# Moving the first image's VectorE work in a fused convolution and attention block

## The chip, the cores and the metric

The kernel runs on one core of one Trainium2 chip. The metric is the device time of one execution in microseconds (us). TensorE (PE in the profile) does the matmuls, VectorE (DVE) the additions, ScalarE (ACT) the activations and copies out of PSUM, GpSimd (POOL) and SyncE (SP) mostly issue transfers.

## The reference, cut to what matters

Eight images of 512 channels by 32x32 pixels, all in f32. Each is group-normalised, goes through one block and is added to the block's input:

```python
t = cbs(x, cv1_w, cv1_bn, 0)              # 1x1 conv 512->512, batch norm, silu
ys = [t[:, :C], t[:, C:]]                 # C = 256
for i in range(N):                        # N = 2
    yi = ys[-1]
    z = cbs(yi, m_cv1_w[i], m_cv1_bn[i], 1)              # 3x3 conv 256->256
    z = bot_attention(z, m_qkv_w[i], m_rw[i], m_rh[i])   # 4 heads of 64, 1024 positions
    z = silu(bn_eval(conv2d(z, m_cv2_w[i], 0), m_cv2_bn[i]))
    ys.append(yi + z)
out = x + cbs(concatenate(ys, axis=1), cv2_w, cv2_bn, 0) # 1x1 conv 1024->512, x is not normalised here
```

## The kernel before

Channels lie on the 128 partitions, so 512 channels are four chunks and 256 are two; a row of 1024 positions is worked in two halves of 512. The program is unrolled over the eight images (b) and the two bottlenecks (n). Every instruction is placed at compile time by a scheduler that takes them in the order of the program as far as their inputs and buffers allow it in its own model; each engine then runs its list in that fixed order. `tc.issue_after(ins)` adds an order: what the block issues on the engine of `ins` comes after `ins`. A tile comes from a pool with a tag and a number of buffers; a new tile of a full tag waits until the oldest readers of one buffer are done.

One image runs so: `group_norm`, `cv1` (1x1), then for each n the 3x3 convolution `conv3x3`, the attention `attention_fast` and the 1x1 `m2` with its residual, and at the end the 1x1 over all parts. While the attention of one bottleneck runs, work of the next image or stage is placed between its groups by the dictionary `behind`: a key g is a group (four of them, each one chunk of channels and one half of the queries), NG and NG + 1 lie behind the last group, -1 ahead of the first. NG is 4.

The 3x3 convolution is done as a product of transformed tiles: `tiles_in` makes the transformed image `v_in` on VectorE (three pairs of rows, for two chunks of input channels), `make_u` makes the transformed filter `u` from the raw 3x3 weights on VectorE (six operations for pair 0 and for pair 1, three and a ScalarE copy for pair 2), the matmuls (L959) run over them, `columns_out` and `rows_out` transform back into z. For output chunk oc, u is needed as three tiles. The filters are made once, in the first image, and stored to DRAM; the later images load them (`load_u`). All of them live in one ring of five buffers of 1 MB (tag "u"), with w1 (weights of cv1), w2, the sums for Strassen's products and their reloaded copies. For n = 0 the filters of chunk 0 are made during the norm, those of chunk 1 during the first convolution. For n = 1, chunk 0 is made ahead of the first attention, chunk 1's pair 2 and pair 0 behind its groups, and pair 1 inside the second convolution (`u_of`).

The products of q, k and v and the two outer 1x1 convolutions are done by Strassen's scheme from the second stage on, with sums of weight blocks. These too are made in the first image, in its second attention: `make_ws` (four sums of 128x1024, behind group 0), `make_sw` (four of 128x512, behind group 1) and `make_sq` (group 2); `make_sq(1)` comes behind the first attention. `project_strassen` begins with the difference t1 of the two halves of z (L644).

At the start the norm of the first image is done in two parts of two chunks each (`group_norm_part`): VectorE's statistics, a small matmul for the group means (`gn_mean`), another for the deviations (`gn_rstd`, read by L510), a power on GpSimd, then one ScalarE activation for each chunk (L529). Between these steps TensorE begins products of cv1 with what is ready (`begin`).

The last image has no next one, so in its attentions `cv2_part` does products of the final 1x1 convolution with y0 and y1 ahead. Its end is `cv2`: for each of eight pieces (an output chunk and a half) the part is added (L1218), silu, the residual piece x_res added (L1221, loaded in pieces of 256 KB into two buffers, L1202) and the piece stored.

Of the kernel before, what the change touches and what calls it, by code (L numbers as in the profile page):

```python
# [61 lines left out]
def kernel(  # L62
# [61 lines left out]
    load_w1_half(0)  # L124
    xs += [load_x(act, 0, c, NX) for c in range(NX // 2, NX)]
# [29 lines left out]
    raws = {(0, 0, 0): load_raw(0, 0, 0, "k")}  # L155

# [20 lines left out]
    def make_ws(w2):  # L177
        (a11, a21), (a12, a22) = ((w[:, :, :CO], w[:, :, CO:]) for w in w2)
        sums = [ring([P, 2, KB, CO], f"s{i}") for i in range(2)]
        s1, s4, s2, s3 = (w[:, j] for w in sums for j in range(2))  # L180
        nc.vector.tensor_tensor(s1, a21, a22, ALU.add)
        nc.vector.tensor_tensor(s2, s1, a11, ALU.subtract)
        nc.vector.tensor_tensor(s3, a11, a21, ALU.subtract)
        nc.vector.tensor_tensor(s4, a12, s2, ALU.subtract)
        last = [nc.gpsimd.dma_start(dst, w) for w, dst in zip(sums, s_dram2)][-1]
        return last, (a11, s1, a12, s4, s2, s3, a22)
# [13 lines left out]

    bn_cv1 = bn_slot(cv1_bn, 2 * NM)
# [3 lines left out]
    for k in range(1, NM):  # L205
        raws[0, 0, k] = load_raw(0, 0, k, "v")
# [152 lines left out]
    def stages(act, small, ps_big, ps_av, n_pt):  # L359
# [134 lines left out]
        def gn_mean(mv, n=NX, pool=ps_big, tag="big"):  # L494

            ps = pool.tile([P, n], F32, tag=tag, name="gm_ps")
            over_groups(ps, mv[:, :, 0])
            gm = small.tile([P, n], F32, tag="gm", name="gm")
            dev = small.tile([P, n], F32, tag="dev", name="dev")
            nc.vector.tensor_copy(gm, ps)  # L500
            nc.vector.tensor_tensor(dev, mv[:, :, 0], gm, ALU.subtract)
            nc.vector.tensor_tensor(dev, dev, dev, ALU.mult)
            nc.vector.tensor_tensor(dev, dev, mv[:, :, 1], ALU.add)
            return gm, dev
# [9 lines left out]
        def group_norm_part(xts):  # L514


            n = len(xts)
            mv = small.tile([P, n, 2], F32, tag="mv", name="mv", bufs=2)
            for c in range(n):
                gn_stats(mv, c, xts[c])  # L520
            yield
            gm, dev = gn_mean(mv, n, ps_av, "av")
            yield
            gr, multiplied, read = gn_rstd(dev, n, ps_av, "av")
            shift = small.tile([P, n], F32, tag="dev", name="shift")
            nc.gpsimd.tensor_tensor(shift, gm, gr, ALU.mult)
            nc.gpsimd.tensor_scalar(shift, shift, -1.0, None, ALU.mult)
            for c in range(n):
                applied = nc.scalar.activation(  # L529
                    xts[c], xts[c], AF.Identity, scale=gr[:, c : c + 1], bias=shift[:, c : c + 1]  # L530
                )
            yield multiplied, read, applied

        def group_norm(xts):

            mv = small.tile([P, NX, 2], F32, tag="mv", name="mv", bufs=2)

            def stats(cs):
                for c in cs:
                    gn_stats(mv, c, xts[c])  # L540

            def apply(cs, gm, gr):
                for c in cs:
                    last = nc.vector.tensor_scalar(
                        xts[c], xts[c], gm[:, c : c + 1], gr[:, c : c + 1], ALU.subtract, ALU.mult
                    )
                return last

            stats(range(NX // 2))
            yield  # L550
            stats(range(NX // 2, NX))
            yield
            gm, dev = gn_mean(mv)
            yield
            yield apply(range(NX), gm, gn_rstd(dev)[0])
# [42 lines left out]
        def project_strassen(n, z, sq, mid):  # L598
# [42 lines left out]
            t = act.tile([P, 4, HALF], F32, tag="pt", name="t_z", bufs=n_pt)  # L641
            t1, t2, t3, t4 = (t[:, i] for i in range(4))
            with tc.issue_after(mid.ins):
                tt(t1, b12, b11, ALU.subtract)  # L644
# [54 lines left out]
        def attention_fast(n, z, at, behind, sq=None, mid=None):  # L699
# [3 lines left out]
            q, kr, vT, later = (*project(n, z), None) if sq is None else project_strassen(n, z, sq, mid)  # L703
# [241 lines left out]
        def conv3x3(n, vs, u_of):  # L945
            z = act.tile([P, NM, HW], F32, tag="z", name="z")
            for oc in range(NM):
# [6 lines left out]
                for i in range(PAIRS):  # L954
# [9 lines left out]
                    if i == 1:  # L964
                        mid = first()
                last()
# [5 lines left out]
            return z, mid  # L972
# [218 lines left out]
        def cv2(b, w2, ys, begun={}, parts={}):  # L1191

            def rows_of(dram, oc, half):
                if isinstance(b, int):
                    return dram[b, ts(oc, P), ts(half, HALF)]
                return dram[bass.ds(b, 1), ts(oc, P), ts(half, HALF)][0]

            def residual(oc, half):  # L1200
                t = act.tile([P, HALF], F32, tag="xr", name="x_res", bufs=2)
                nc.gpsimd.dma_start(t, rows_of(x, oc, half))  # L1202
                return t

            pieces = [(oc, half) for oc in range(NO) for half in range(NH)]
            res = [residual(*pieces[0]), residual(*pieces[1])]
            for i, (oc, half) in enumerate(pieces):
                if half == 0:
                    ks = range((2 + N) * NM)
                    if oc in begun:  # L1210
                        ps = cv2_products(w2, ys, oc, ks[-NM:], begun[oc], by_half=oc == NO - 1)
                    else:
                        ks = ks[2 * NM if oc in parts else 0 :]
                        ps = cv2_products(w2, ys, oc, ks, ends=(ks[0], ks[-1]), by_half=oc == NO - 1)
                t = act.tile([P, HALF], F32, tag="t" if i + 2 < len(pieces) else "h", name="t", bufs=2)
                src = ps[:, half, :]
                if oc in parts:
                    nc.vector.tensor_tensor(t, src, parts[oc][:, ts(half, HALF)], ALU.add)  # L1218
                    src = t
                silu(t, src, bn_cv2 + oc)  # L1220
                nc.vector.tensor_tensor(t, t, res.pop(0), ALU.add)  # L1221
                q = nc.sync if isinstance(b, int) and i + 2 >= len(pieces) and b == B - 1 else nc.gpsimd
                q.dma_start(rows_of(out, oc, half), t)
                if i + 2 < len(pieces):
                    res.append(residual(*pieces[i + 2]))
# [26 lines left out]
    s.table_of(AF.Silu)  # L1252
# [7 lines left out]
    with tc.issue_after(read.ins):  # L1260
        next(norm)
    begun = {}
# [6 lines left out]
    with tc.issue_after(first.ins):  # L1269
        next(norm)  # L1270
# [7 lines left out]
    made = make_u(2, u_first[2][:, 0], raws[0, 0, 0])  # L1278
    with tc.issue_after(normed.ins):
        made = make_u(0, u_first[0][:, 0], raws[0, 0, 0])  # L1280
    with tc.issue_after(made.ins):
        nc.vector.tensor_scalar(rstd, bnp[:, :, 3], BN_EPS, None, ALU.add)
        nc.gpsimd.tensor_tensor(rstd, rstd, mhalf[:, :NBN], ALU.pow)
        make_u(1, u_first[1][:, 0], raws[0, 0, 0])
        made = make_u(0, u_first[0][:, 1], raws[0, 0, 1])
# [19 lines left out]
    for b in range(B):  # L1305
# [6 lines left out]
        def u_of(n):  # L1312
            def of(oc):
                nonlocal last_load
                if b == 0 and oc == 1:
                    if n == 0:
                        with tc.issue_after(last.ins):
                            for i in range(PAIRS):
                                make(n, oc, [i])
                    else:  # L1320
                        for k in range(NM):
                            raws[n, oc, k] = load_raw(n, oc, k, "kv"[k])
                        with tc.issue_after(last.ins):
                            make(n, oc, [1])
# [8 lines left out]
        z, mid = s.conv3x3(0, vs, u_of(0))  # L1333
# [49 lines left out]
        def second():  # L1383
            if b == 0:
                make_sq(1, "xr", 2)
            if six:
# [3 lines left out]
            else:  # L1390
                parts[2] = s.cv2_part(w1, (y0, y1), 2)
# [7 lines left out]
        ao, check = s.attention_fast(0, z, b * N * NM * NH, behind, sq.get(0), mid)  # L1399
        last = s.m2(0, ao, y1, lambda oc, half: inner(y2, oc, half))  # L1400
# [4 lines left out]
        else:  # L1405
            parts[3] = s.cv2_part(w1, (y0, y1), 3)
            parts[0] = s.cv2_part(w1, (y0, y1), 0, range(NM))
# [5 lines left out]
        z, mid = s.conv3x3(1, vs, u_of(1))  # L1413
        w2 = ws = three = stored = halves = None
# [8 lines left out]
        def prepare():  # L1423
            nonlocal stored, ws
            stored, ws = make_ws(w2)

        def ahead():
            nonlocal w2, three
            if b == 0:
                make_sw(halves)  # L1430
# [25 lines left out]
        if b == 0:  # L1456
            behind |= {-1: load_ahead, 0: prepare, 2: lambda: make_sq(0, "x", NX)}
        if six:
            behind |= {(1, 1): six[3], (2, 1): six[4]}
        ao, check = s.attention_fast(1, z, (b * N + 1) * NM * NH, behind, sq.get(1), mid)  # L1460
# [105 lines left out]
```

## Time and profile before

| what | us |
|---|---|
| median of 4 runs (2327.52 to 2330.09) | 2329.1 |
| the profiled execution | 2329.56 |
| its span in the profile | 2328.0 |
| TensorE busy | 2294.1 |
| VectorE busy | 1837.3 |
| ScalarE busy | 986.4 |
| first matmul of cv1 starts | 12.09 |
| last matmul of cv2 ends | 2319.0 |

The profile is that of one execution. A line number (L959) is the line of the kernel that issued an instruction. Matmuls on f32 appear as two records each. Times in the timeline are us from the start of the span; "idle before <- X" says that the engine was idle for so long and that X ended it. The granted clock of TensorE is 1.00 when it runs at full speed.

### The profile page before, as it was taken

The numbers are of one execution on the slowest core, as the hardware profiler recorded it, in microseconds if no ns is written. First come the engines' busy times: TensorE is split into PE (matmuls) and PEld (weight loads), VectorE is DVE, ScalarE is ACT, GpSimd is POOL, SyncE is SP. The second block draws the span as 40 slices with busy tenths as digits, with TensorE's granted clock in tenths as the row PEclk, the third lists the DMA queues.
The fourth block names the chain that finished last, engine by engine and source line by source line (L and its number), as shares of the span: only waits on it lengthen the run. The fifth ranks groups of instructions, "written<-read, shape, count | busy, mean of one in ns | idle before, by whom it ended". The sixth has DMA issues, their size and how long they took to land.

```text
span 2328.0 us, 36527 instructions
## 1 busy us (share of the span) xinstructions
PE 2294.1 (99%) x14806; PEld 1175.9 (51%) x14806; DVE 1837.3 (79%) x2918; ACT 986.4 (42%) x1287; POOL 91.0 (4%) x312
## 2 busy tenths in 40 slices
PE   7999999999999999999999999999999999999998
PEld 4546346373464635546364463645536364473643
DVE  7878877879778887888778877888877888777674
ACT  2443524536245361544525445253542535335352
POOL 1000000000000000000000000000000000000001
PEclk9999999999999999999999999999999999999999
DMA  7423215041340414304152131602216031250202
GB/s 237 172 67 112 107 62 227 16 145 38 102 184 15 150 33 154 135 15 148 40 203 81 54 106 51 245 32 87 73 47 249 29 126 34 68 217 16 86 11 70
DMA packets 95441, 235.60 MB, mean 101 GB/s; under 512 B 28064, under 2 KB 50528, under 8 KB 81824
## 3 DMA queue, kind: packets, MB, share of 16 engines
q1 hardware_dynamic: 83456, 182.84, 23.0%
q0 software_dynamic: 11808, 50.34, 5.6%
q8 instruction: 119, 1.95, 0.3%
q14 instruction: 58, 0.48, 0.1%
HBM read 198.54 MB, written 34.60 MB: 100 GB/s over the span
## 4 chain that ended last, share of the span: by engine, by line
PE 94%; DVE 5%; DMA 1%; ACT 0%; issue 0%; POOL 0%; DVEq 0%; ACTq 0%
PE av_ps L758 19%; PE l_ps L724 18%; PE c_ps L959 14%; PE c L1014 8%; PE p_ps L617 8%; PE x_ps L1126 6%; PE c_new L1014 6%; PE m_ps L980 5%; PE ps L381 3%; PE pv_ps L621 3%; PE s_ps L776 1%; PE p_ps L621 1%; PE s_ps L794 1%; DVE acc L744 1%; DVE v_in L440 0%
## 5 line engine op out<-in xcount | busy, mean ns | idle before, releaser
L728 ACT ACTIVATE pt<-l_ps 128x1024 f32<-128x1024 f32 x512 | 494.9, 1023 | 414.4 <-PE l_ps L724 387.2
L744 DVE TENSOR_TENSOR acc<-acc,pt 128x1024 f32<-128x1024 f32 x384 | 469.5, 1223 | 69.0 <-ACT pt L728 43.2
L758 PE MATMUL av_ps<-pt,vT 64*64 64x512 f32 x4096 | 488.2, 593 | 0.5 <-DVE ao L766 0.5
L724 PE MATMUL l_ps<-q,kr 64*64 64x512 f32 x4096 | 486.7, 591 | 0.0
L959 PEld LDWEIGHTS c_ps<-v_in,u 128*128 128x128 f32 x2720 | 306.3, 192 | 7.9 <-issue 6.7
L959 PE MATMUL c_ps<-v_in,u 128*128 128x128 f32 x2720 | 306.9, 275 | 1.1 <-DVE v_in L440 1.1
L758 PEld LDWEIGHTS av_ps<-pt,vT 64*64 64x64 f32 x4096 | 159.3, 133 | 270.6 <-issue 226.5
L724 PEld LDWEIGHTS l_ps<-q,kr 64*64 64x64 f32 x4096 | 160.2, 133 | 264.7 <-issue 253.5
L447 ACT COPY m<-c_ps 128x256 f32<-128x256 f32 x96 | 35.5, 370 | 227.1 <-PE c_ps L959 223.9
L1014 PE MATMUL c_new<-t_in,ws 128*128 128x512 f32 x288 | 124.6, 592 | 0.0
L980 PE MATMUL m_ps<-ao,m_sb 128*128 128x512 f32 x256 | 112.5, 592 | 0.0
L742 DVE TENSOR_TENSOR acc<-pt 128x1024 f32<-128x1024 f32 x64 | 78.1, 1220 | 20.9 <-ACT pt L728 20.9
L364 ACT ACTIVATE m_kept<-m_kept,bh,sh 128x512 f32<-128x512 f32 x42 | 31.9, 806 | 146.0 <-DVE m_kept L1098 86.3
L617 PE MATMUL p_ps<-t_z,sq 128*128 128x512 f32 x180 | 88.0, 599 | 2.0 <-issue 2.0
L1014 PEld LDWEIGHTS c_new<-t_in,ws 128*128 128x128 f32 x288 | 54.7, 190 | 68.9 <-issue 66.0
L364 ACT ACTIVATE t<-m_ps,bh,sh 128x512 f32<-128x512 f32 x64 | 48.1, 776 | 83.9 <-PE m_ps L980 82.5
L980 PEld LDWEIGHTS m_ps<-ao,m_sb 128*128 128x128 f32 x256 | 48.6, 190 | 61.2 <-issue 61.2
L988 DVE TENSOR_TENSOR ylast<-t,ypad 128x512 f32<-128x512 f32 x32 | 22.0, 692 | 63.3 <-ACT t L364 63.3
L364 ACT ACTIVATE z<-z,bh,sh 128x512 f32<-128x512 f32 x64 | 48.6, 806 | 52.5 <-DVE z L476 52.4
L440 DVE TENSOR_TENSOR v_in<-w_rows 128x512 f32<-128x512 f32 x96 | 66.2, 689 | 0.0
L1014 PE MATMUL c<-ypad,ws 128*128 128x512 f32 x144 | 63.8, 592 | 0.0
L448 DVE TENSOR_TENSOR r_mid<-c_ps,m 128x256 f32<-128x256 f32 x64 | 27.2, 424 | 45.9 <-ACT m L447 45.9
(255 smaller groups left out, 3010.2 us busy)
## 6 DMA issues: line engine op xcount, KB each, us to landing
u<-u SPq DMA_DIRECT2D x85, 1024.0 KB
x<-in_x_dram SPq DMA_DIRECT2D x32, 512.0 KB
x_res<-in_x_dram POOLq DMA_DIRECT2D x28, 512.0 KB, 6.7
out_dram<-m_kept POOLq DMA_DIRECT2D x28, 512.0 KB, 7.3
u<-u_new POOLq DMA_DIRECT2D x12, 1024.0 KB, 6.1
w<-in_cv_w_dram SPq DMA_DIRECT2D x12, 1024.0 KB
rs<-r_dram SPq DMA_DIRECT2D x96, 128.0 KB
ws<-s SPq DMA_DIRECT2D x24, 512.0 KB
```

The source lines that it names most:

```text
L364: return nc.scalar.activation(dst, src, AF.Silu, scale=sh[:, k : k + 1], bias=bh[:, k : k + 1])
L617: nc.tensor.matmul(ps[:, o, :], w[:, o, :], rhs, start=not onto, stop=True, skip_group_check=onto)
L621: nc.tensor.matmul(v[:, ts(j, P)], rhs[:, ts(j, P)], w[:, 2, :], start=j == 0 and not onto, stop=True, skip_group_check=True,)
L724: nc.tensor.matmul(ps[kh * HD : (kh + 1) * HD, hd, :], kr[r, c, o : o + HD], q[r, c, ts(half, HALF)], start=True, stop=True,)
L728: exp = nc.scalar.activation(pt[:, i], ps, AF.Exp, scale=SCALE)
L742: return nc.vector.tensor_tensor(accs[g], pt[:, 0], pt[:, 1], ALU.add)
L744: ins = nc.vector.tensor_tensor(accs[g], accs[g], pt[:, i], ALU.add)
L758: nc.tensor.matmul(avs[g][hd * HD : (hd + 1) * HD, kh, :], vT[r, j, o : o + HD], pt[r, i, hd, :], start=(j == 0), stop=(j == NJ - 1),)
L959: nc.tensor.matmul(ps[:, row, col, :], us[i][:, k, row, SLOT[col], :], vs[i][:, k, row, col, :], start=(k == 0), stop=(k == NM - 1),)
L980: nc.tensor.matmul(pss[oc][:, half, :], m2_sb[:, n, k, ts(oc, P)], ao[:, k, ts(half, HALF)], start=(k == 0), stop=(k == NM - 1),)
L1014: nc.tensor.matmul(ps[:, o, :], w[:, k, ts(o, P)], rhs[part][:, c, :], start=(k == 0 and not onto), stop=(k == KB - 1), skip_group_check=onto,
L1126: nc.tensor.matmul(ps[:, o, :], w[:, c, ts(o, P)], rhs[c], start=(c == 0 and not onto), stop=(c == 1), skip_group_check=onto,)
```

## The change

1. At the start, the raw filter of the first chunk is loaded ahead of half of w1 and of x's last two chunks, and the second raw filter ahead of the batch norm parameters. The filter sums of input chunk 0 go into the norm: pair 2 ahead of the second part's statistics, pair 0 ahead of its mean, pair 1 behind its mean. The norm's ScalarE activations are done in halves.
2. Pair 1 of the second bottleneck's chunk 1 is made right behind the first attention, and the additions of `m2` are ordered behind it.
3. Strassen's sums in the second attention: three sums of `make_ws` behind group 1, the fourth with `make_sq(0)` behind group 2, `make_sw` behind group 3.
4. t1 of `project_strassen` is traced inside the convolution.
5. In the last image, the part of chunk 0 with y0 alone goes behind the last group, and those of chunks 2 and 3 behind `m2`.
6. `cv2` loads the residual in whole chunks (512 KB), and its last chunk is worked in pieces of 512, 256 and 256 columns.

```diff
+    raws = {(0, 0, 0): load_raw(0, 0, 0, "k")}     # moved ahead of the next two
     load_w1_half(0)
     xs += [load_x(act, 0, c, NX) for c in range(NX // 2, NX)]
...
     def make_ws(w2):
+        def part1():
             nc.vector.tensor_tensor(s1, a21, a22, ALU.add)
             nc.vector.tensor_tensor(s2, s1, a11, ALU.subtract)
             nc.vector.tensor_tensor(s3, a11, a21, ALU.subtract)
+        def part2():
             nc.vector.tensor_tensor(s4, a12, s2, ALU.subtract)
+            return [nc.gpsimd.dma_start(dst, w) for w, dst in zip(sums, s_dram2)][-1]
...
             for c in range(n):
+                for half in range(NH):
+                    part = xts[c][:, ts(half, HALF)]
+                    applied = nc.scalar.activation(part, part, AF.Identity, scale=gr[:, c : c + 1], ...)
...
                     if i == 1:
                         mid = first()
+                        if oc == NM - 1 and summed:
+                            with tc.issue_after(mid.ins):
+                                t = first_sum(z)
...
     with tc.issue_after(read.ins):
+        with tc.issue_after(loaded.ins):
+            made = make_u(2, u_first[2][:, 0], raws[0, 0, 0])
         next(norm)
+    with tc.issue_after(made.ins):
+        made = make_u(0, u_first[0][:, 0], raws[0, 0, 0])
...
-    with tc.issue_after(first.ins):
-        next(norm)
+    with tc.issue_after(first.ins), tc.issue_after(made.ins):
+        averaged = next(norm)
+    with tc.issue_after(averaged.ins):
+        made = make_u(1, u_first[1][:, 0], raws[0, 0, 0])
...
-    made = make_u(2, u_first[2][:, 0], raws[0, 0, 0])
-    with tc.issue_after(normed.ins):
-        made = make_u(0, u_first[0][:, 0], raws[0, 0, 0])
     with tc.issue_after(made.ins):
         nc.vector.tensor_scalar(rstd, bnp[:, :, 3], BN_EPS, None, ALU.add)
         nc.gpsimd.tensor_tensor(rstd, rstd, mhalf[:, :NBN], ALU.pow)
-        make_u(1, u_first[1][:, 0], raws[0, 0, 0])
         made = make_u(0, u_first[0][:, 1], raws[0, 0, 1])
...
             def of(oc):
-                    else:
-                        for k in range(NM):
-                            raws[n, oc, k] = load_raw(n, oc, k, "kv"[k])
-                        with tc.issue_after(last.ins):
-                            make(n, oc, [1])
...
         def second():
             if b == 0:
                 make_sq(1, "xr", 2)
+                for k in range(NM):
+                    raws[1, 1, k] = load_raw(1, 1, k, "kv"[k])
...
-                parts[2] = s.cv2_part(w1, (y0, y1), 2)
+                parts[0] = s.cv2_part(w1, (y0, y1), 0, range(NM))
...
+        made = make(1, 1, [1]) if b == 0 else None
+        with tc.issue_after(made.ins) if made else nullcontext():
             last = s.m2(0, ao, y1, lambda oc, half: inner(y2, oc, half))
...
-            parts[3] = s.cv2_part(w1, (y0, y1), 3)
-            parts[0] = s.cv2_part(w1, (y0, y1), 0, range(NM))
+            for oc in (2, 3):
+                parts[oc] = s.cv2_part(w1, (y0, y1), oc)
...
         def prepare():
-            stored, ws = make_ws(w2)
+            stored = to_dram()
+            make_sq(0, "x", NX)
         def ahead():
             if b == 0:
-                make_sw(halves)
+                ws, sums, to_dram = make_ws(w2)
+                sums()
...
-            behind |= {-1: load_ahead, 0: prepare, 2: lambda: make_sq(0, "x", NX)}
+            behind |= {-1: load_ahead, 2: prepare, 3: lambda: make_sw(halves)}
...
-            def residual(oc, half):
-                t = act.tile([P, HALF], F32, tag="xr", name="x_res", bufs=2)
+            def residual(oc):
+                t = act.tile([P, HW], F32, tag="xr", name="x_res", bufs=2)
...
+                final = isinstance(b, int) and oc == NO - 1
+                sizes = (HALF, HALF // 2, HALF // 2) if final else (HALF, HALF)
```

## The prediction

> **What bounds the kernel.** I read the page first, then what TensorE (PE) waited for, then the windows round each wait, then the timeline there.
>
> ```profile
> span 2328.0 us, 36527 instructions
> PE 2294.1 (99%) x14806; PEld 1175.9 (51%) x14806; DVE 1837.3 (79%) x2918; ACT 986.4 (42%) x1287; POOL 91.0 (4%) x312
> ```
>
> TensorE is busy 99%: only its 34 us of gaps, and the time it runs at a low clock after them, can be won. The waits of TensorE (total, times, longest) name them:
>
> ```profile
> PE gm_ps L491 <- DVE mv L484: 7.5, 1, 7.5
> PE c_ps L959 <- DVE u_new L331: 4.7, 1, 4.7
> PE s_ps L776 <- DVE acc L744: 4.3, 1, 4.3
> ...
> PE p_ps L617 <- issue: 2.0, 1, 2.0
> PE c_ps L959 <- DVE v_in L440: 1.1, 1, 1.1
> ```
>
> Each happened once. The timeline puts them at 0 to 12 us (norm), 54.4 (filter sums of the second output chunk late), 250 (softmax additions late behind Strassen's sums), 213 (t_z) and 2188.6 (last image). Between 330 and 2140 us there is none. The windows show what follows a gap (column after POOL: granted clock):
>
> ```profile
> 50.00:60.00 10.00, 5.28 (x44) 5.09 (x42) 10.00 (x28) 2.11 (x4) 0.00 (x0) 0.95 0.00 0
> 59.00:66.00 7.00, 6.60 (x30) 6.34 (x31) 7.00 (x20) 2.18 (x4) 0.53 (x1) 0.51 0.36 144
> 213.00:220.00 7.00, 5.00 (x16) 3.08 (x15) 5.29 (x12) 4.29 (x7) 0.00 (x0) 0.76 0.00 0
> 249.00:261.00 12.00, 7.69 (x52) 2.18 (x48) 11.55 (x13) 2.62 (x4) 0.84 (x2) 0.72 0.43 175
> ```
>
> After the gaps at 54, 213 and 250 the clock is half for about 6.8, 3.4 and 6.8 us; half of that is lost.
>
> **The change, part by part.** The sum is made against the profiled execution's 2329.56 us (span 2328.0); the median of the runs is 2329.1. Minus is a gain.
>
> *Start.* The first matmul waits at 12.09 for a 1.19 us activation of x (128x1024). In halves the first piece is done about 0.5 us sooner (a 128x512 copy is 0.60, a 128x512 activation 0.81). The raw filter (576 KB) now goes ahead of half of w1 and of x2, x3: at the 320 to 400 GB/s of the first 10 us they land about 1.8 us later. That and 1.3 us of sums ahead of x2's statistics are hidden: these ended at 12.35 and TensorE took their mean at 15.79, 3.4 us later. Without that cover it would cost the excess. On POOL, rstd's pow (3.16 us) must not come ahead of the norm's: their slack is 2 us (x2 ready 24.6, wanted 26.0). Value **-0.5**, bounds -2.2 (the clock rises one window earlier) and +3.
>
> *Filter sums in the norm's gaps.* VectorE was idle 2.1 us before 16.2 and 4.0 before 21.0; from 21.0 to 59 it never rests, and TensorE's gap at 54.4 ends when its sum L331 ends. Twelve operations leave that stretch: pair 0 (3.1 us, 21.07 to 24.2), pair 1 (2.4, half of twelve interleaved operations in 4.9). So all behind comes 5.5 us sooner. The gap cost 4.7 + 0.3 idle and 3.3 of clock, 8.3. It is not all won: the middle pair's last sum ends at 66.7, now 61.2, and TensorE, restarting at 53.9 at full clock, wants it from 57.5. Some 2.8 us stay, clock included. Value **-5.5**, bounds -8.3 and -2 (only pair 0 fits, because the norm's read L510 is queued inside pair 1). SP's blocked load (L140, 8.2 us until raw is free) also goes sooner.
>
> *Filter sums behind the first attention.* They leave the second convolution, which removes the t_z gap: 2.0 idle and 1.7 of clock, **-3.7** (bounds -3.7 and 0). But the new place adds a wait. These sums write a new tile of the five-slot ring "u". At the end of the first attention all five are taken: w1, three filters for chunk 0 and pair 0 of chunk 1. The trace shows the ring full:
>
> ```profile
> 154.85 1.44 SPq L140 DMA_DIRECT2D raw<-in_m_cv_w_dram  x2
> ...
> 174.35 0.69 DVE L988 TENSOR_TENSOR ypad<-t,ypad 128x512 f32<-128x512 f32 x1 [6.79 <-ACT t L364]
> 175.06 13.90 PE L381 MATMUL ps<-x,w 128*128 128x512 f32 x32
> ...
> 188.79 14.68 PE L959 MATMUL c_ps<-v_in,u_new 128*128 128x128 f32 x130
> ...
> 192.20 0.56 DVE L334 SCALAR_TENSOR_TENSOR u_new<-raw 128x384 f32<-128x384 f32 x1
> ```
>
> The raw data were called for at 154.85, yet the sum L334 came only after w1's last matmul (188.95), and the next filter load waited 6.5 us more, for the convolution to give up a slot:
>
> ```profile
> SPq L344 <- PE c_ps L959: 6.5, 1, 6.5
> ```
>
> The slot that comes free is w1's, after cv1's chunks of y0, which TensorE runs behind m2. And m2's additions (L988) are now queued behind these sums on VectorE, with tiles_in behind them, for which the convolution waits. Worked out: m2's accumulators stay held (its last activations need the buffers that L988 frees), so cv1's second chunk has to wait for the first's two activations, 1.6 us; w1 is free at 188.95 + 1.6 = 190.55. Twelve sums, 4.9 (as at 24.18 to 29.1): 195.6. From the first L988 to both chunks of the first v_in took 174.35 to 183.9, 9.55 us, some 1.0 of it waiting for ACT: 8.6, so the convolution starts at 204.2 instead of 188.9, 15.3 late. The clock after 13.7 us of idling is half for 3.4 to 6.8 us: 2.6. The 1.6 us gap may drop it too (1.1 at 2188.6 did not, 2.0 at 213 did): 0.6. Value **+18.5**, bounds 13 (no clock loss, no held accumulator) and 22; 0 if a slot were free. The store of u goes ahead of w_rows' memsets on POOL, which wait for v_in anyway.
>
> *Strassen's sums spread.* At 250 VectorE has behind it, within one group, 2.4 us of later(), and four 1.22 us sums. Now groups 1, 2, 3 get 3.4, 3.0 and 2.5. Every later image puts 3.4 us of 128x1024 sums on groups 1 and 2 of the same attention, without one wait. So the 4.3 and 3.0 of clock go: **-7.3**, bounds -7.3 and 0.
>
> *First Strassen sum.* In the later images it already runs right behind L470 (374.78), and TensorE waits for nothing: 0. Cover gone: 0.6 us each, with z's activations behind it.
>
> *Last image.* c_ps' 1.1 us goes, since 3.4 us more of matmuls lie ahead of it: **-1.1**. The 3.4 taken from under the last softmax sums are spare by 0.9 (scale done 2163.0, m2 would want it at 2163.9); with that cover gone m2 would wait. The end:
>
> ```profile
> 2317.11 1.88 PE L381 MATMUL ps<-ylast,w 128*128 128x512 f32 x4
> ...
> 2322.52 0.69 DVE L1221 TENSOR_TENSOR t<-t,x_res 128x512 f32<-128x512 f32 x1 [1.23 <-DMA x_res<-in_x_dram]
> ```
>
> The last residual is called for about 6 us before its use in one 512 KB piece (256 KB took 3.2), on POOL behind two stores. The 1.23 wait goes and the last store is half as long: **-1.6**, bounds -2.2 and +1.5 (an additional 2 to 3 us of landing).
>
> Sum: -0.5 - 5.5 + 18.5 - 3.7 - 7.3 - 1.1 - 1.6 = -1.2. That is 2328.4 against the profiled execution, **2327.9** against the median.
>
> [...] At 213 a gap of 2.0 us halved the clock for 3.4 us, so I price it at 3.7. [...]
>
> **Rivals.** (a) The ring wait does not arise: the scheduler finds a slot, or the sums do not hold up m2. Then 18.5 falls away: 2309.4. For it: only the order at one place decides. Against: L334 and L344 above. (b) Slower: the softmax additions stay late. The 3.4 us of ws sums fall on group 1, which begins with what group 0 left undone: its first addition came 2.4 late (238.1) and later() takes 2.4; each pair gives back 1.1 (3.44 of TensorE against 2.3 of additions). If more than about 1 us is carried over, group 1's row sums wait as at 250, 7.3: 2335.2. Against: the later images. (c) The change does not do what it says, the sums not landing in the gaps, or an unforeseen wait: +3 to +9.
>
> **How the numbers follow.** Forecast 0.55, its own range 2321 to 2334; (a) 0.17; (b) 0.15; (c) 0.13. A measurement tells 0.2%, 4.7 us, from no change: below 2324.4 is faster, above 2333.8 slower. Forecast: 0.11 faster, 0.41 same, 0.03 slower. (a) is all faster; (b) 0.12 slower, 0.03 same; (c) 0.10 slower, 0.03 same. Together 0.28, 0.47, 0.25. The range 2308 to 2336 leaves out part of (a), (b) and (c), under 2 in 10.
>
> **What would show it.** A TensorE wait of 13 to 14 us in the second convolution, ended by v_in, with L334 right behind w1's last matmul, says the ring step is right; no wait there says (a). The waits on L331 (4.7) and L744 (4.3) should be gone or under 2.5. A wait on L744 says (b). The end from the last product should shorten from 9.1 to 7.5. The prediction is wrong if the large wait lies elsewhere.

## The result, and the profile after

The kernel after took 2332.07 us (median of 40 runs, 2330.29 to 2333.45), the kernel before 2328.68 (60 runs). The ratio is 1.0014, with a 95% interval of 1.0010 to 1.0019: 3.4 us slower, where 1.2 faster was forecast. Two profiled executions lie less far apart, 2329.56 and 2331.59. That of before was 0.9 above its median and that of after 0.5 below, which makes the 1.4 between the two differences.

The page of after, span and busy times:

```profile
span 2330.1 us, 36531 instructions
PE 2290.6 (98%) x14806; PEld 1176.6 (50%) x14806; DVE 1838.9 (79%) x2920; ACT 987.5 (42%) x1292; POOL 88.9 (4%) x308
```

TensorE's work is the same 14806 records. It is busy 3.5 us less than before, because less of it runs at half clock (8.0 us of its busy time against 15.8, each program's end not counted), and the span is 2.1 us longer. So TensorE waits 5.6 us more, and its waits (total, times, longest) say where:

```profile
PE c_ps L970 <- DVE v_in L445: 13.4, 3, 11.4
...
PE c_ps L970 <- DVE u_new L344: 3.2, 1, 3.2
```

The 4.3 on acc, the 2.0 ahead of t_z and the 1.1 of the last image are gone. The 4.7 on u_new has become 3.2. New is the 13.4 on v_in. The timeline has the chain that makes it, and at its ends the two places where less was won than forecast:

```profile
11.80 1.29 DVE L488 BATCH_NORM_STATS2 st<-x 128x6 f32<-128x512 f32 x2 [1.20 <-DMA x<-in_x_dram]
20.59 0.16 DVE L515 TENSOR_SCALAR gr<-gv_ps 128x2 f32<-128x2 f32 x1 [1.77 <-PE gv_ps L496]
...
180.28 7.13 PE L386 MATMUL ps<-x,w 128*128 128x512 f32 x16 [1.54 <-ACT y L369]
187.46 1.03 DVE L339 SCALAR_TENSOR_TENSOR u_new<-raw 128x384 f32<-128x384 f32 x2 [23.24 <-DMA w_half<-in_cv_w_dram]
192.28 1.29 DVE L1002 TENSOR_TENSOR ypad<-t,ypad 128x512 f32<-128x512 f32 x2
198.81 0.77 PE L970 MATMUL c_ps<-v_in,u_new 128*128 128x128 f32 x2 [11.39 <-DVE v_in L445]
200.93 9.36 PE L970 MATMUL c_ps<-v_in,u_new 128*128 128x128 f32 x64 [1.35 <-DVE v_in L445]
...
2323.72 2.29 SPq L1240 DMA_DIRECT2D out_dram<-t  x3
```

Read it from 180: w1's last product ends at 187.4, after a 1.54 wait for its accumulator. At once L339 runs, VectorE having stood 23.24 us with m2's additions (L1002) queued behind it. These run from 192.28, tiles_in after them, and the convolution starts at 198.81.

To place the differences I took each matmul record's start in after, minus that of the same record in before. The last column is the forecast's own term.

| place in before (us) | offset goes from to | step | forecast |
|---|---|---|---|
| 0 to 22 | 0 to -0.4 | -0.4 | -0.5 |
| 54 to 66 | -0.4 to -3.4 | **-3.0** | -5.5 |
| 168 to 212 | -3.4 to +14.7 | +18.1 | +18.5 |
| 213 to 220 | +14.7 to +10.8 | -3.9 | -3.7 |
| 250 to 261 | +10.9 to +3.6 | -7.3 | -7.3 |
| 2188 | +3.7 to +2.4 | -1.3 | -1.1 |
| last matmul to the end | +2.4 to +2.1 | **-0.3** | -1.6 |

Between these places the offset drifts by 0.2 in all.

### The profile page after: what moved, and what is told of

Its sections match the earlier page's. It is cut to its first block, busy times and chain, and to the rows that moved or that the text cites. A ratio compares the mean times of both kernels' runs of the same rounds, so it can differ in the third digit from the quotient of the medians.

```text
span 2330.1 us, 36531 instructions
## 1 busy us (share of the span) xinstructions
PE 2290.6 (98%) x14806; PEld 1176.6 (50%) x14806; DVE 1838.9 (79%) x2920; ACT 987.5 (42%) x1292; POOL 88.9 (4%) x308
## 4 chain that ended last, share of the span: by engine, by line
PE 95%; DVE 4%; ACT 0%; DMA 0%; POOL 0%; issue 0%; DVEq 0%; ACTq 0%
PE av_ps L768 19%; PE l_ps L734 19%; PE c_ps L970 14%; PE c L1028 8%; PE p_ps L630 8%; PE x_ps L1140 6%; PE c_new L1028 6%; PE m_ps L994 5%; PE ps L386 4%; PE pv_ps L634 3%; PE s_ps L786 1%; PE p_ps L634 1%; PE s_ps L804 1%; DVE acc L754 0%; DVE v_in L445 0%; PE v_ps L595 0%
## 5 line engine op out<-in xcount | busy, mean ns | idle before, releaser
L1002 DVE TENSOR_TENSOR ylast<-t,ypad 128x512 f32<-128x512 f32 x32 | 22.0, 693 | 63.2 <-ACT t L369 63.2
```

## The experiments

The theory: the wait for the ring's slot cost 18.1 and hid some 16 us of gains. Two gains were smaller than forecast. The first runs test the wait, the next the parts alone and the two small gains, the last what really limits the first convolution. "Before" in this section is that of the same chip in the same session (2327.9 to 2329.3).

**1. Pair 1 back inside the second convolution.**

```diff
-        made = make(1, 1, [1]) if b == 0 else None      # behind the first attention
+        made = None
...
 # in u_of(1), as before:
+                    with tc.issue_after(last.ins):
+                        make(n, oc, [1])
```

> The kernel after, with pair 1 of the second bottleneck's chunk 1 made back inside the second convolution, as before. Theory (the new tile waits for a slot of the ring "u", and m2's additions wait behind it): TensorE's waits of 13.4 us on v_in go, 18.1 us by the offset of the same matmuls, and the gap ahead of t_z comes back, 4.2: 2332.1 - 18.1 + 4.2 = 2318.2. Rival (the convolution waits because VectorE is late for other reasons, the sums being only what stands there): v_in is still late by most of the 13 us, about 2330.

Measured: 2316.72 (ratio to before 0.9948, interval 0.9934 to 0.9962). The wait on v_in is gone. What came back at the t_z place were two waits at full clock (the mean over the run is 0.998, over before 0.995), 1.0 on u_z and 0.9 on z:

```profile
PE p_ps L630 <- ACT u_z L659: 1.0, 1, 1.0
...
PE p_ps L630 <- ACT z L369: 0.9, 1, 0.9
```

With that place undone the rest of the change is a gain of 11.8.

**2. The tile outside the ring.**

```diff
-                    us[oc, i] = new_u("u_new")
+                    if (n, oc, i) == (1, 1, 1):
+                        us[oc, i] = act.tile([P, NM, 2, NC, P], F32, tag="q", name="u_new")
+                    else:
+                        us[oc, i] = new_u("u_new")
```

> The kernel after, with the tile of that pair 1 outside the ring: in the buffer of q, which nobody needs between the first attention and the second projection. Everything else and the order behind the sums stay. Theory (a slot of the ring is what was missing): the sums run at about 155 to 164 us, as soon as their raw filters have landed, the convolution starts as before, and the t_z gap stays away: 2332.1 - 18.1 = 2314.0. Rival A (VectorE waited for a transfer, the half of w1 that the profile names as the releaser of L339, or for the raw filters): the sums still start at 187 and the time stays at 2332. Rival B (the order alone costs, the sums' own 4.9 us ahead of m2's additions): about 2319.

Measured: 2313.81 (0.9935, 0.9922 to 0.9949), 18.3 less than after. The timeline of this kernel:

```profile
156.65 0.56 DVE L339 SCALAR_TENSOR_TENSOR u_new<-raw 128x384 f32<-128x384 f32 x1 [2.39 <-DMA raw<-in_m_cv_w_dram]
184.63 18.03 PE L970 MATMUL c_ps<-v_in,u_new 128*128 128x128 f32 x160
```

The sums start 31 us sooner, when their raw filter lands, and the convolution runs without a gap. The order is the one of after; so neither the order alone nor a transfer was at fault. In after, the profile names the half of w1 as what ended L339's wait. That load goes into another buffer (tag "x"), and in run 2 the sums ran before it was even called for, at 179.7; in after it merely was the last event before. A named releaser is a candidate, to be tried.

**3. The ring as it is, without the order.**

```diff
-        with tc.issue_after(made.ins) if made else nullcontext():
+        with nullcontext():
             last = s.m2(0, ao, y1, ...)
```

> The kernel after, with the tile in the ring as it is, but without the order that puts m2's additions behind the sums. Theory (the slot comes free only behind w1's last matmul, at about 187 us, and it costs only because m2's additions are queued behind the wait): the sums still start at about 187, but the additions run at 171 to 182, so the convolution starts as before; with the sums between tiles_in's last pieces its third pair of v_in may come up to 2 us late: 2314 to 2317. Rival (the ring's wait is long enough to hold the convolution by itself, whatever stands behind it): still above 2325.

Measured: 2316.30 (0.9947, 0.9933 to 0.9960). The sums still wait, until 186.11, but the additions are done by then. TensorE's waits keep one line of it:

```profile
PE c_ps L970 <- DVE v_in L445: 2.7, 1, 2.7
```

So the 18 us need both: a tile whose slot comes late, and a queue made to wait behind it. Either cure alone brings back 15.8 or more.

**4. The move alone, on the kernel before.**

> The kernel before, with this one edit alone: pair 1 of the second bottleneck's chunk 1 made right behind the first attention, m2's additions ordered behind it. Theory: + 18.1 for the wait and - 4.2 for the gap ahead of t_z: 2328.7 + 13.9 = 2342.6. Rival (the wait came of several edits together, since they all move VectorE's order): within 3 us of 2328.7.

Measured: 2341.58 (1.0057, 1.0044 to 1.0071), 13.1 slower than before, against 13.9. By the offsets the wait costs 18.1 and the t_z gap gives 3.9 back, as in after.

**5. The norm's read behind pair 1's sums** (on the kernel of run 2).

```diff
-    with tc.issue_after(first.ins):
+    with tc.issue_after(first.ins), tc.issue_after(made.ins):
         multiplied, normed, applied = next(norm)
```

> The kernel with the tile outside the ring (2313.8), and one instruction moved on VectorE: the norm's read of gv_ps (L515) comes behind pair 1's six sums and no longer behind the first of them. Theory (that read stops VectorE for 1.77 us and leaves five of pair 1's six sums behind it, which is why the norm's gaps take in only half of the sums): the sums fill the 1.77, the read comes 0.7 later, which x's activations can spare, everything behind it on VectorE runs 1.8 earlier, and TensorE's wait on u_new at 54 us falls from 3.2 to about 1.4. Gaps of 1.1 to 1.6 left the clock alone, so the half clock behind it, 1.7, goes too: 2312.0 to 2310.3. Rival (the sums that end that wait are late because z's sums of chunk 0 are queued ahead of them): the wait stays at 3 and the time at 2313.8.

Measured: 2314.46 (0.9936, 0.9922 to 0.9949): nothing won, the theory missed. The timeline says why:

```profile
22.32 2.90 POOL L1307 TENSOR_TENSOR rstd<-rstd,mhalf 128x16 f32<-128x16 f32 x1
25.76 2.93 ACT L536 ACTIVATE x<-x,shift,gr 128x512 f32<-128x512 f32 x4 [11.15 <-POOL shift L532]
31.84 0.69 DVE L422 SCALAR_TENSOR_TENSOR w_tmp<-ypad 128x512 f32<-128x512 f32 x1 [1.49 <-ACT ypad L369]
```

The read came 0.5 later, and on GpSimd the batch norm's power slipped in ahead of the shift. So x was activated 2.9 later, TensorE waited 0.97 for it, and VectorE stood for ypad instead of for gv_ps.

**6. Two stores at the end** (on the kernel of run 2).

```diff
-                sizes = (HALF, HALF // 2, HALF // 2) if final else (HALF, HALF)
+                sizes = (HALF, HALF)
```

> The kernel with the tile outside the ring (2313.8), and the last chunk worked in two pieces of 512 columns instead of 512, 256, 256: two stores on SP, the residual still in whole chunks. Theory (the third store's issue, 0.7 to 1.7 us where the two ahead of it took 0.36 and 0.37, gave back what the residual's early arrival won): the last store's issue ends 3.9 us behind the start of the last matmul instead of 4.6 to 5.6: 2313.8 - 1.0 = about 2312.8. Rival (the end waits for the last piece to land, whatever its issue takes; with 256 KB in place of 128 KB that is longer): 2313.8 to 2314.5.

Measured: 2312.93 (0.9930, 0.9916 to 0.9943). SP's issues at the end:

```profile
2305.99 1.05 SPq L1240 DMA_DIRECT2D out_dram<-t  x2
```

The last issue ends 4.0 us behind the start of the last product, against 5.6 in run 2 and 5.2 in after. From the start of the last product to the end of the span, the four kernels with two whole pieces and the early residual took 9.07 to 9.35 us (9.2 on average), the five with three pieces 9.32 to 10.24 (9.8), and the four with the end of before 9.6 to 11.1 (10.2). The rival has a part in it: from the end of the last issue to the end of the span it is 5.1 to 5.4 us with two pieces and 4.1 to 4.9 with three, so most of what the issue gains is lost behind it and about 0.5 stays. The medians of runs 2 and 6 differ by 0.9, less than the width of their intervals: the row agrees with the theory, the times alone don't settle it.

**7. The start alone, on the kernel before.**

> The kernel before with the start alone: the order of the first loads, the filter sums of input chunk 0 inside the norm, the activations in halves. Theory: what the trace after showed there, -0.5 and -2.9, in all 2328.5 - 3.4 = 2325.1. Rival (the part is worth the 6.0 that I gave it, and something else in the kernel after took 2.6 back): 2322.5.

Measured: 2323.06 (0.9976, 0.9967 to 0.9985; 11 runs), 5.6 below the 60-run median of before and 6.2 below that of its session. The rival's number came true, but not for its reason: its wait on u_new is the same 3.2 as in after, and the offset behind it is -4.6, with -1.2 of it from the start and -3.4 from the sums. Two later gaps that this kernel still has add -1.7 and -1.5, and its end, 1.5 longer than that of before, takes 1.5 back. These are windows of its profile (granted clock in the column after PE's busy time, the only engine kept):

```profile
206.82:210.23 3.41, 1.79 (x11) 1.00 0.00 0
244.37:247.78 3.41, 0.00 (x0) 1.00 0.97 394
247.78:251.19 3.41, 3.04 (x20) 0.50 0.19 78
251.19:254.60 3.41, 3.41 (x36) 1.00 0.02 1
```

and of the kernel before:

```profile
212.57:215.98 3.41, 1.41 (x8) 1.00 0.00 0
215.98:219.40 3.42, 3.42 (x11) 0.50 0.00 0
```

The t_z gap, 2.0 in both, lowered the clock in before, where it lies in one window, and not here, where two windows share it (1.62 in the first). The wait on acc, 4.3 in both, was followed by 3.4 us at half clock here and by 6.8 in before. Both are luck: they come from where the windows lie in this execution. Nine of the 11 runs took 2322.3 to 2323.9 and two 2325.9 and 2327.5; whether the nine had this luck no run shows, so that part of the 5.6 stays open.

**8. Strassen's sums alone, on the kernel before.**

> The kernel before with Strassen's sums in the second attention spread alone (three sums of make_ws behind group 1, the fourth with make_sq behind group 2, make_sw behind group 3). Theory: TensorE's wait on acc (4.3) and the half clock behind it go: 2328.5 - 7.1 = 2321.4. Rival (VectorE is only early enough there because other edits relieved it; alone, group 1's row sums wait instead): within 2 us of 2328.5.

Measured: 2321.86 (0.9970, 0.9959 to 0.9981), 7.4 less than before. The wait on acc is gone with no other edit's help, and no other wait on the softmax sums has come.

**9. The read behind the sums, the power behind the shift** (on the kernel of run 6).

```diff
-    with tc.issue_after(first.ins):
+    with tc.issue_after(first.ins), tc.issue_after(made.ins):
         multiplied, normed, applied = next(norm)
...
-    with tc.issue_after(made.ins):
+    with tc.issue_after(made.ins), tc.issue_after(normed.ins):
+        made = make_u(0, u_first[0][:, 1], raws[0, 0, 1])
         nc.vector.tensor_scalar(rstd, bnp[:, :, 3], BN_EPS, None, ALU.add)
         nc.gpsimd.tensor_tensor(rstd, rstd, mhalf[:, :NBN], ALU.pow)
-        made = make_u(0, u_first[0][:, 1], raws[0, 0, 1])
```

> The kernel with two stores (2312.9), with the norm's read of gv_ps behind pair 1's six sums as in the run before, and the batch norm's power (2.9 us on POOL) kept behind the norm's shift. Theory (with the read moved alone, that power slipped between the norm's power and its shift, x's activations came 2.9 late, TensorE waited 0.97 for x, and VectorE, done with its sums, stood 1.49 for ypad): no wait on x any more; VectorE is 1.3 earlier at the first w_tmp, but ypad lets it start at about 30.9 instead of 31.6, so the wait on u_new falls from 3.2 to about 2.6: 2312.3. Rival (VectorE's queue alone sets the wait, ypad does not hold it): 1.8 less wait and no half clock, 2309.4 to 2311.1.

Measured: 2314.32 (0.9942, 0.9928 to 0.9955). TensorE waits for x no more, so GpSimd's order was the cause in run 5. But the wait on u_new is still 3.3, for VectorE now stands for the power:

```profile
27.12 0.18 DVE L1310 TENSOR_TENSOR sh<-bnp,rstd 128x16 f32<-128x16 f32 x1 [2.36 <-POOL rstd L1308]
```

VectorE's idle time from 9.2 to 31.5 us is 7.1 in before, 4.05 in after, 3.9 in run 5 and 4.7 here. The seven kernels with the start of after have 3.4 to 4.6 and the three with that of before 5.7 to 7.1, so runs 5 and 9 lie with the seven: the idle time changes its releaser and not its size.

**10. Chunk 0's back transform behind chunk 1's sums** (on the kernel of run 6).

```diff
+                if ahead:                                # first image, n = 0, oc = 0
+                    with tc.issue_after(later([1, 2]).ins):    # chunk 1's sums
+                        first()
+                        last()
```

> The kernel with two stores (2312.9), with the back transform of the first convolution's chunk 0 (rows_out: L473 to L481, 3.3 us of VectorE) behind chunk 1's filter sums, and the last columns_out of chunk 0 behind pair 0's. Theory (TensorE's wait at 54 us is set by what stands ahead of chunk 1's sums on VectorE, which never rests from 31 us on; the sums taken out of that queue early on were too few): pair 0 is done 2.3 earlier, pair 1 at 59.8 instead of 63.3, the wait falls from 3.2 to about 0.9, too short to lower the clock: 2312.9 - 2.3 - 1.7 = 2308.9, up to 2310 if TensorE then waits 1.1 for pair 1. Rival (z of chunk 0 is needed as soon as it comes, so the projection waits for what was put behind): 2312.9 or more, with a new wait at about 73 us.

Measured: 2314.97 (0.9944, 0.9931 to 0.9958). The wait at 54 us did go (0.16 left), and TensorE ran 5.3 ahead of run 6 by 62 us (0.6 of it stems from ahead of 54 us). By 78 us it was 0.5 behind. The waits of this kernel show where it went:

```profile
PE ps L386 <- ACT z L369: 1.9, 1, 1.9
...
PE v_ps L595 <- DVE r_ends L456: 0.9, 1, 0.9
PE c_ps L970 <- DVE u_new L344: 0.7, 2, 0.5
```

The wait has moved to z, behind the convolution, and the clock fell there instead: the eight 128x512 records behind the 1.9 take 5.40 us, the eight ahead of it 3.67. The rival, not the theory, had this right.

**11. Runs 9 and 10 together.**

> The edits of the last two together. Theory: the 0.6 of the first comes on top of the second as long as TensorE still waits at 54 us: 2308.3 to 2309.4. Rival (ypad's arrival or pair 1's sums hold it by then): the same time as the second alone.

Measured: 2315.02 (0.9943, 0.9929 to 0.9956): again no gain, with the same waits on z (1.9) and v_ps (0.9).

The lowest median is that of run 6: after with its one tile outside the ring and two stores at the end, 2312.93, which is 0.7% below before and 19 us below after. The times don't tell it from run 2.

## Why the prediction was right and wrong

**The ring wait** was the step that everything hung on, and it held. Forecast: cv1's second chunk waits 1.6 for its accumulator (1.54 in the trace), the sums run right behind w1's last matmul, and the convolution idles 13.7 (11.39 + 1.35 + 0.64 = 13.4). The half clock lasted 13.65 us by the windows, from 191.4 to 205.0; TensorE worked in about 4.9 of them and lost 2.4 (forecast 2.6). Runs 2 and 3 show the two conditions, run 4 the price by itself. A slip in the sum does not matter: 190.55 + 4.9 is 195.45, not 195.6. Rival (a) is in effect the kernel of run 2: 2309.4 was its forecast, 2313.8 its time, and most of the difference is the two terms below.

**Right too:** t_z's gap (-3.9 in the trace of after; 2.9 by the times of runs 1 and 2, since the half clock behind it doesn't always come: not in runs 1 and 7), Strassen's sums (rival (b) is out: run 8), the last image, the start.

**The first step that failed: "Value -5.5"** for the filter sums in the norm's gaps. It measured -3.0. The prediction took all twelve sums as gone from the stretch behind 21 us. Its own weaker bound had the reason: the read L515 is queued inside pair 1. Only its first sum ran ahead of the read and VectorE stood 1.77 for it; another 1.20 was spent waiting for x2, whose load now comes behind the raw filter's 576 KB. In the kernel before, VectorE rested twice there, and the sums were to fill these rests:

```profile
16.22 0.16 DVE L500 COPY gm<-gm_ps 128x2 f32<-128x2 f32 x1 [2.13 <-PE gm_ps L491]
21.00 0.16 DVE L510 TENSOR_SCALAR gr<-gv_ps 128x2 f32<-128x2 f32 x1 [4.03 <-PE gv_ps L491]
```

So VectorE's idle time fell by 3.1 in these two executions (2.3 by the averages of run 9's section, 6.3 and 4.0) and not by 5.5. The middle pair's last sum, forecast to end at 61.2 instead of 66.7, ended at 63.2 in after:

```profile
62.80 0.45 DVE L345 SCALAR_TENSOR_TENSOR u_new<-u_new 128x256 f32<-128x256 f32 x1
```

TensorE got what VectorE got: its wait shrank by 1.5, and one half window of 3.4 us, worth 1.7, went. Behind the sizing is a wrong picture. I priced TensorE's gap at 54 us as the thing to win. Run 10 took that gap away and won nothing: from 31.5 to 75 us, when z is done, VectorE idles 1.0 us in all in after and not at all in run 10, and TensorE waits for z if not for u. This fits a stretch whose bound is the sum of VectorE's work, where only time that VectorE itself wins can count. Runs 5 and 9 meant to win such time and did not, so no run shows that winning it would pay in full.

**The second: "Value -1.6"** for the tail. It measured -0.3. The wait for x_res is gone as forecast and the last addition ends 1.2 sooner behind the last matmul. But the third store's issue took 1.36 us, where the two ahead of it took 0.36 and 0.37, and ended 5.21 behind the start of the last product, against 5.19 in before, whose two stores are

```profile
2321.32 2.26 SPq L1223 DMA_DIRECT2D out_dram<-t  x2
```

I had counted a shorter piece and put the third issue at nothing. The -0.3 is that of two executions; the averages of run 6's section (10.2 and 9.8) make it about -0.5. Run 6 takes the third issue away, and the averages then come to -1.0, still short of -1.6.

Together the two make 3.8; the other steps came out 0.5 better than forecast. -1.2 + 3.3 = +2.1, by which the span grew. The rest up to the measured 3.4 is where the two profiled executions lie against their medians. The sign hung on the difference of two large numbers, a wait of 18.5 and gains of 19.7, so an error of 1.2 in any term could turn it.

**The price of t_z's gap**, 3.7, was read from one row; the offset fell by 3.9 there. The half-clock stretches begin and end a multiple of 3.41 us behind the first rise: 12, 14, 58, 59, 69 and 71 such windows in before (59.0 - 18.0 = 41.0 us is 12), 12, 13, 51 and 55 in after. The t_z gap of 2.0 us, lying in one window of before, was followed by one window at half clock, which the prediction priced at 1.7.

## What to carry to other kernels

Before a step is moved ahead, count the slots of the buffer it writes into at the new place, and name what is queued behind it there; a late slot costs little by itself (2.5 us by the times of runs 2 and 3) and much when the path stands behind it (18.3 by those of after and run 2). A gap of the busiest engine may be a gain only if the engine that ends it has time to win: look at what that engine does after the gap until it next rests (run 10 took 3.2 us of wait away and won nothing). Count a transfer's issue as well as its bytes when it is the last thing in the program (the third store's took 1.36 us in after).

## What the runs showed of the hardware

*The clock.* I divided the thirteen profiled executions into windows of 3.41 us from the first rise of each. The clock fell at the end of a full-speed window in which TensorE had idled 1.86 us or more (20 windows, the fall at each program's end not counted; 2.00 at 212.57 in before, 2.75 at 54.86 in after), and never after one with 1.63 or less (1.62 at 206.82 in run 7, 1.54 at 177.74 in after). It rose again behind every window with 0.37 or less idle (0.37 at 247.78 in run 7), and behind none with 0.81 or more (0.81 at 253.53 in before); in between (0.42 to 0.48, three windows; 0.42 at 58.97 in before, no rise) both happened. At half clock 128x512 records start 0.85 us apart, at full clock 0.43 (216.14 and 216.99, 219.92 and 220.35 in before). So the same gap costs its own length (t_z's 2.0 in run 7), or about 1.7 us more (the same 2.0 in before, acc's 4.3 in run 7) or 3.4 more (the 4.3 in before), by where the windows lie. And that changes between executions: cv1's first matmul started at 11.8 to 12.6 us in each, the first rise came anywhere from 14.95 to 18.0. The kernels of before, run 4 and run 8 start with the same program, and their first matmul came at 12.03 to 12.09; the rise came at 18.02, 14.95 and 16.08.

*The third store in a row.* In the five kernels with three stores on SP whose starts lie 0.46 us apart, the first two issues took 0.36 and 0.37 us and the third 0.71, 1.36, 1.53, 1.72 and 2.13. With two stores the second took 0.35. The second piece is as small as the third (256 columns), so the size alone does not do it; whether the place or the short distance between the starts does (0.70 us with two whole pieces) was not tried.
